# A graph attention layer on one core: ten chunks of edges in place of eleven

## The chip, the cores and the metric

The kernel runs on 1 core of one Trainium2 chip. The metric is the time on the device, in microseconds (us). Three runs of the kernel before gave 5710.31, 5714.75 and 5733.31 us; their median is 5714.75. The profile shows one more execution, recorded by the hardware profiler, which took 5704.97 us, with a span of 5703.2 us from its first to its last instruction.

The engines are called as in the profile: PE is the matrix engine (PEld its weight loads), DVE the vector engine, ACT the scalar engine, POOL the GpSimd engine, SP the engine whose queue issues most transfers. L1192 is line 1192 of the kernel.

## The reference

There are 12500 nodes of 128 features and 412500 edges with 64 features each, sorted by `dst`. The sources `src` are spread at random. Cut to what matters, the reference computes:

```
n      = relu(layernorm(x))                       # 12500 x 128
h,q,k,v = n@Wn+bn, n@Wq+bq, n@Wk+bk, n@Wv+bv
eh     = edge_attr @ We + be                      # 412500 x 128
hmid   = leaky_relu(concat(q[src], k[dst], eh) @ A1 + b1, 0.2)
scores = leaky_relu(hmid @ A2 + b2, 0.2)          # 8 heads
w      = softmax(scores.mean(-1), over all edges)
out    = segment_sum(w[:, None] * v[dst], src)
y      = h + out
result = x + gamma*(y - mean(y))/sqrt(var(y)+eps) + beta
```

The edges come in the order of `dst`, and the sums go by `src`. So the kernel has to bring the edges into another order on the way.

## The kernel before

**The work in tiles.** The edges make 403 *groups* of 1024, and a group has 8 tiles of 128 edges. The nodes, as sources, make 98 *blocks* of 128: the block of an edge is `src` mod 98, its place in the block the quotient.

**The first stage** (`first_stage`, from L953) goes through the groups in order. For a group SP loads the edge features (`ea_t`, L966), a window of 42 nodes' k and v (`kv`, L971) and the edges' positions in that window (`offs`, L974). DVE turns the positions into a selection (`sel`, L984). In four half steps PE multiplies the features by the folded weights (L1007) and adds the selected k and v (L1010), ACT takes the result out of PSUM into a ring of rows (L991, L994), and POOL scatters the rows to a table in DRAM (`tab`, L924), 8 scatters of 128 rows to a group. A row has 257 numbers: the place in the block, 128 of the hidden layer and 128 of v.

**The second stage** (`second_stage`, from L1023) goes through the blocks. The table has room for so many tiles of each block. A *unit* is as many blocks as make at most 12 tiles: three blocks of 4 tiles, four of 3 or four of 2. For a unit SP loads the rows (`rows_of`, L1038), the queries of its blocks (`qw`, L1049) and the spread places (`pls`, L1068). The work goes by *quads* of four tiles. PE turns four tiles (L1088) and adds the queries by a selection (L1093): three matmuls, one for each of three parts of q, and for each block that the quad touches. ACT and DVE make the leaky relu (L1102, L1103). For each unit come the heads (L1110), the scores (L1118 to L1161) and a running maximum. Then DVE builds the weighted selection of each tile (L1179; in the last chunk ACT builds one tile of each quad, L1184 and L1185), PE multiplies it by v (L1192), and DVE adds the sums of the unit to the accumulator of all nodes, faded to the new maximum (L1208).

**Chunks.** So that both stages run at once, the groups are cut into chunks, and each chunk has its own part of the table, three parts in rotation (`TABS`). The table of numbers `CHUNKS` (L72) gives for each chunk its number of groups and the least number of tiles for each block. `tiles_of` (L157) raises that number where the edges still to come would not fit. What a block has beyond the places of its chunk goes on into the next chunk's part. Edges that find no place at all would go through a slow loop over all groups at the end (`other_edges`, L1299); the trace shows none of it.

**Slots.** Before a chunk's edges can be scattered, each needs its slot in the table. `ready(c)` (L641) finds them: `count` makes a histogram of the blocks (L467, L474), `plan` sets what is carried over, and `place_slots` ranks the edges within their blocks (L572, L579, L635), five tile columns at a time.

**The order.** The program is one order for each engine, written by `interleave` (L80): in the loop over stages (L1421 to L1453) stage c mixes the first stage of chunk c, the second stage of chunk c-1 and `ready(c+1)`, each in proportion to its number of steps. Stage 0 has no blocks to work on; there the node projections and the index work of all chunks go beside. After the last chunk's groups only its blocks are left: the *tail*. Two waits tie the stages together: the load of a block's rows waits for the last scatters of its chunk, and the first scatter of a chunk waits until the part of the table that it takes over has been read. At the start of stage 0 zeros are written to places that may stay empty in the second and third part (`clear_ends`, L226).

Of the kernel before, what the change touches and what calls it, by code (L numbers as in the profile page):

```python
# [68 lines left out]
AHEAD = 140  # L69
LEAD = 4  # L70
SURE = 3.75
CHUNKS = ((57, 4), (43, 4), (43, 4), (43, 3), (33, 3), (33, 3), (33, 3), (33, 3), (33, 3), (33, 3), (19, 2))  # L72
BECAUSE = "worked out within these bounds on the chip"


def _ceil(a, b):
    return -(-a // b)
# [44 lines left out]
def kernel(ctx: ExitStack, tc: tile.TileContext, n_edges, x, src, dst, ea, w_nv, w_qt, w_kt,  # L122
# [22 lines left out]
    g0 = 0  # L145
    whole = sum(n for n, _ in CHUNKS)
    for i, (n, _) in enumerate(CHUNKS):
        n = NG - g0 if i == len(CHUNKS) - 1 else max(1, round(NG * n / whole))
        chunks.append((g0, n))
# [4 lines left out]
    for c in reversed(range(NC)):  # L154
        mean = sum(means[c:])
        needed = mean + SURE * mean ** 0.5 - P * sum(tiles_of)
        tiles_of.insert(0, max(_ceil(int(needed) + 1, P), CHUNKS[c][1]))  # L157
    chunks = [(g0, n, t, NTN * t) for (g0, n), t in zip(chunks, tiles_of)]
# [1387 lines left out]
```

## Time and profile before

| | |
|---|---|
| median of three runs | 5714.75 us |
| the profiled execution | 5704.97 us, span 5703.2 us |
| PE busy | 4378.4 us, 77% of the span |
| DVE busy | 4076.2 us, 71% |
| POOL busy | 3239.9 us, 57% |
| ACT busy | 1897.7 us, 33% |
| mean granted clock of PE | 0.879 of full speed |
| moved by DMA | 1316.75 MB, 231 GB/s on the mean |

Busy shares are of the whole span, and the stages differ; the view of stretches gives the same numbers for a stretch of time. A line of the view of groups has the line, engine, operation, names and shapes with their count, then busy time and mean ns of one, then the idle time before them and what ended it. Matmuls overlap in their pipeline, so the sum of their busy time is not the time that PE needs. A scatter's time on POOL is that of issuing it; its transfer comes after.

### The profile page before, as it was taken

Reading aid. Unit: us, or ns where it says so; the run is one execution under the profiler, and the core shown is the slowest. Engines: PE = TensorE matmul, PEld = TensorE weight load, DVE = VectorE, ACT = ScalarE, POOL = GpSimd, SP = SyncE. Lnnn points to the kernel's source line nnn. Section 1 sums busy time; section 2 is a strip of 40 time slices with the busy share of each in tenths; the row PEclk is TensorE's granted clock in tenths of the full one; section 3 lists DMA queues with packets and bytes.
Section 4 is the critical chain, followed back from the end, with each engine's and each line's share of the span. In section 5 each row is a group of like instructions: output and inputs, shape, how many; then the busy total and the mean of one; then the engine's idle time right before and its main releaser. Section 6 shows DMA issues by size and latency. Waiting matters only on the chain. (4 is left out here: it accounts for less than half of the span.)

```text
span 5703.2 us, 86990 instructions
## 1 busy us (share of the span) xinstructions
PE 4378.4 (77%) x26559; PEld 3030.7 (53%) x26559; DVE 4076.2 (71%) x12996; ACT 1897.7 (33%) x5104; POOL 3239.9 (57%) x3250
## 2 busy tenths in 40 slices
PE   6766647877777777777777877778777787778898
PEld 3333324555555555555555555555555555556674
DVE  7777526776777666667776767777777776667898
ACT  2333322333333333333333333333333333333346
POOL 3666566665566555665655655665655665665510
PEclk8888768998898888888888988888989888989999
DMA  4667767777777777776777767777776776778985
GB/s 134 202 196 218 212 208 226 243 246 224 226 241 234 224 225 241 236 234 222 239 227 232 244 224 239 231 242 232 245 236 215 247 237 210 253 236 273 304 280 198
DMA packets 711378, 1316.75 MB, mean 231 GB/s; under 512 B 152208, under 2 KB 362309, under 8 KB 710889
## 3 DMA queue, kind: packets, MB, share of 16 engines
q1 hardware_dynamic: 492080, 867.97, 52.1%
q0 software_dynamic: 154704, 424.26, 20.1%
q10 hardware_dynamic: 64105, 18.76, 1.4%
q8 instruction: 214, 3.51, 0.3%
q14 instruction: 275, 2.25, 0.1%
HBM read 820.50 MB, written 490.10 MB: 230 GB/s over the span
## 5 line engine op out<-in xcount | busy, mean ns | idle before, releaser
L924 POOL DMA_INDIRECT tab<-row,slots x3223 | 3236.7, 1004 | 2211.9 <-ACT row L994 979.8
L1192 PE MATMUL o_ps<-rows_of,w 128*128 128x128 f32 x6860 | 1020.7, 292 | 313.4 <-DVE w L1179 170.0
L1192 PEld LDWEIGHTS o_ps<-rows_of,w 128*128 128x128 f32 x6860 | 913.5, 201 | 440.3 <-issue 258.8
L994 ACT ACTIVATE row<-row_ps 128x512 f32<-128x512 f32 x1151 | 681.2, 593 | 1126.1 <-PE row_ps L1010 343.4
L1102 ACT ACTIVATE low<-h_ps 128x512 f32<-128x512 f32 (+1 forms) x861 | 511.8, 594 | 1438.6 <-remote 432.6
L1007 PE MATMUL row_ps<-w_ea,ea_t 128*128 128x256 f32 x2302 | 821.6, 442 | 188.0 <-ACT row L994 127.0
L1179 DVE TENSOR_SCALAR w<-iota_f,rows_of,score 128x128 f32<-128x128 f32 x3381 | 954.6, 357 | 0.1
L1103 DVE TENSOR_TENSOR rows_of<-h_ps,low 128x512 f32<-128x512 f32 (+1 forms) x861 | 589.1, 684 | 497.5 <-ACT low L1102 335.0
L1093 PE MATMUL h_ps<-sel_q,qw 128*128 128x128 fp8e4 (+3 forms) x4242 | 766.9, 314 | 5.4 <-issue 5.2
L1007 PEld LDWEIGHTS row_ps<-w_ea,ea_t 128*128 128x128 f32 x2302 | 425.8, 214 | 420.9 <-issue 186.3
L1110 PE MATMUL s_ps<-rows_of,a_sb 128*32 128x384 f32 (+2 forms) x2392 | 314.7, 604 | 384.4 <-DVE rows_of L1103 257.2
L1088 PE MATMUL h_ps<-ident,rows_of 128*128 128x128 f32 x3430 | 580.1, 295 | 5.8 <-issue 5.8
L1010 PEld LDWEIGHTS <-sel 126*128 126x128 fp8e4 x3224 | 344.2, 107 | 298.4 <-issue 77.7
L1088 PEld LDWEIGHTS h_ps<-ident,rows_of 128*128 128x128 f32 x3430 | 455.1, 154 | 83.0 <-issue 44.4
L1010 PE MATMUL row_ps<-kv,sel 126*128 126x256 bf16 x2302 | 489.1, 296 | 7.0 <-issue 4.6
L1093 PEld LDWEIGHTS <-qw 128*128 128x128 bf16 x4242 | 412.5, 104 | 134.7 <-issue 39.8
L635 DVE TENSOR_REDUCE num<-run 128x5 f32<-128x490 f32 (+1 forms) x648 | 425.9, 657 | 6.4 <-PE run L579 2.2
L994 ACT ACTIVATE row<-t_bank 128x512 f32<-128x512 f32 x461 | 273.5, 593 | 465.9 <-PE t_bank L1010 190.6
L579 PE MATMUL run<-one,rest_b 128*128 128x500 f16 x637 | 263.1, 413 | 210.8 <-DVE num L635 127.9
L984 DVE TENSOR_SCALAR sel<-offs,third 126x512 fp8e4<-126x512 uint8 x806 | 365.4, 494 | 64.9 <-remote 31.8
L1078 DVE TENSOR_SCALAR sel_q<-pls,part 128x512 fp8e4<-128x512 uint8 (+1 forms) x837 | 367.7, 492 | 0.0
L1148 DVE TENSOR_SCALAR_CACHE_REDUCE s_ps<-s_ps,less_of 128x128 f32<-128x128 f32 x298 | 105.9, 355 | 365.6 <-PE o_ps L1192 114.7
(249 smaller groups left out, 4420.3 us busy)
## 6 DMA issues: line engine op xcount, KB each, us to landing
rows_of<-tab SPq DMA_DIRECT2D x264, 1542.0 KB
ea_t<-in_ea SPq DMA_DIRECT2D x403, 256.0 KB
qw<-q_tab SPq DMA_DIRECT2D x192, 384.0 KB
tab<-row,slots POOLq DMA_INDIRECT x3223
offs<-off_d SPq DMA_DIRECT2D x403, 126.0 KB
pls<-pl_d SPq DMA_DIRECT2D x264, 192.0 KB
rows_of<-tab SPq DMA_DIRECT2D x27, 1028.0 KB
qw<-q_tab SPq DMA_DIRECT2D x96, 288.0 KB
```

Source lines behind the costliest of these rows:

```text
L635: nc.vector.tensor_reduce(num, strips[:, :NTN, :m].rearrange("p b m -> p m b"), AX.X, ALU.max)
L924: i = nc.gpsimd.indirect_dma_start(out=tab[:, :], out_offset=bass.IndirectOffsetOnAxis(ap=slots[c][t // (8 * STR)][:m, t % (8 * STR):t % ( ...
L994: nc.scalar.activation(row[:, :, 1:ROW], bank, AF.Copy)
L1007: nc.tensor.matmul(bank[:, :, 0:D], lhsT=ea_g[:, ts(k, P)], rhs=w_ea, start=True, stop=False, skip_group_check=True)
L1010: nc.tensor.matmul(bank[:, b, :], lhsT=sel[:, ts(b * halves + k, P)], rhs=kv, start=False, stop=True, skip_group_check=True)
L1078: nc.vector.tensor_scalar(sel[:, a:b], plss[i][:, a:b], part1, None, op0=ALU.is_equal, saturate=False)
L1088: nc.tensor.matmul(h_ps[:, ts(j, P)], lhsT=rows_of[i][:, a + j, 1:D + 1], rhs=ident, is_transpose=True, start=j == 0, stop=False, skip_gro ...
L1093: nc.tensor.matmul(h_ps[:, (x0 - a) * P:(x1 - a) * P], lhsT=qws[i][:, s, ts(k, D)], rhs=plss[i][:, x0 * P:x1 * P], start=False, stop=k == ...
L1102: nc.scalar.activation(low, h_ps, AF.Copy, scale=SLOPE)
L1103: nc.vector.tensor_max(rows_of[i][:, a:b, 1:D + 1], h_ps.rearrange("p (j e) -> p j e", j=m), low.rearrange("p (j e) -> p j e", j=m))
L1179: nc.vector.tensor_scalar(w, iota_f, rows_of[i][:, t, 0:1], state["score", i][:, t:t + 1], op0=ALU.is_equal, op1=ALU.mult)
L1192: nc.tensor.matmul(state["o_ps"][:, ts(t // ct, D)], lhsT=w, rhs=rows_of[i][:, t, D + 1:ROW], start=t == 0, stop=t % ct == ct - 1, skip_gr ...
```

## The change

Only the table of chunks changes:

```diff
-CHUNKS = ((57, 4), (43, 4), (43, 4), (43, 3), (33, 3), (33, 3), (33, 3), (33, 3), (33, 3), (33, 3), (19, 2))
+CHUNKS = ((57, 4), (46, 4), (46, 4), (45, 4), (45, 4), (45, 4), (45, 4), (33, 3), (24, 2), (17, 2))
```

The first number is the groups, the second the tiles of a block. Both tables have 403 groups and 35 tiles for each block. Before, three chunks had blocks of four tiles, seven of three and one of two; now it is seven, one and two. Through `interleave` this moves every instruction from stage 1 on. Two places show how.

On PE, in stage 5, a quad of chunk 4 before. Its blocks have three tiles, so a quad touches two blocks:

```order
L1088 MATMUL h_ps<-ident,rows_of 128x128 x4
L1093 LDWEIGHTS qw
L1093 MATMUL h_ps<-sel_q,qw 128x128
L1093 LDWEIGHTS qw
L1093 MATMUL h_ps<-sel_q,qw 128x128
L1093 LDWEIGHTS qw
L1093 MATMUL h_ps<-sel_q,qw 128x128
L1093 LDWEIGHTS qw
L1093 MATMUL h_ps<-sel_q,qw 128x384
L1093 LDWEIGHTS qw
L1093 MATMUL h_ps<-sel_q,qw 128x384
L1093 LDWEIGHTS qw
```

A sixth matmul of 384 columns ends it. With the change a quad there is one block of four tiles:

```order
L1088 MATMUL h_ps<-ident,rows_of 128x128 x4
L1093 LDWEIGHTS qw
L1093 MATMUL h_ps<-sel_q,qw 128x512
L1093 LDWEIGHTS qw
L1093 MATMUL h_ps<-sel_q,qw 128x512
L1093 LDWEIGHTS qw
L1093 MATMUL h_ps<-sel_q,qw 128x512
```

Three matmuls of 512 columns stand for six that have as many columns together.

On SP's queue, late in the program, in the last stage that still has groups. Before this is stage 10, with 19 groups and the blocks of chunk 9, three tiles each (771 numbers of a partition are three rows of 257; `ea_t`, `kv` and `offs` belong to a group, the others to a unit):

```order
L1038 DMA rows_of<-tab 128x4x771
L1068 DMA pls<-pl_d 128x1536
L1049 DMA qw<-q_tab 128x1536
L966 DMA ea_t<-in_ea 128x512
L971 ISA
L971 DMA kv<-kv_tab 126x256
L974 DMA offs<-off_d 126x1024
L1038 DMA rows_of<-tab 128x4x771
```

With the change it is stage 9, with 17 groups and the blocks of chunk 8, two tiles each:

```order
L1038 DMA rows_of<-tab 128x4x514
L1049 DMA qw<-q_tab 128x1536
L1068 DMA pls<-pl_d 128x1024
L1038 DMA rows_of<-tab 128x4x514
L966 DMA ea_t<-in_ea 128x512
L971 ISA
L971 DMA kv<-kv_tab 126x256
L974 DMA offs<-off_d 126x1024
L1049 DMA qw<-q_tab 128x1536
L1068 DMA pls<-pl_d 128x1024
L1038 DMA rows_of<-tab 128x4x514
```

The units there are smaller, two quads instead of three, and a load of the queries belongs to two quads instead of three.

## The prediction

> **What bounds the kernel now.** I read the page first, then the busy time stage by stage, because the change only moves work between stages.
>
> ```profile
> span 5703.2 us, 86990 instructions
> ...
> PEclk8888768998898888888888988888989888989999
> ```
>
> No engine is full over the span, so the stages have to be seen apart. Stage c forms and scatters the rows of chunk c, works on the blocks of chunk c-1 and finds the slots of chunk c+1. Its end is the last scatter of its chunk. The view of stretches below has one row for each stage, from stage 0 to stage 10, then the tail. The columns are the length, then busy time and count on PE, PEld, DVE, ACT and POOL, then clock, DMA share and GB/s. The count on POOL is 8 per group (344 for 43 groups, 264 for 33, 151 for 19).
>
> ```profile
> core 0: us, PE busy (x) PEld busy (x) DVE busy (x) ACT busy (x) POOL busy (x), PEclk, DMA share, GB/s
> 72.00:810.00 738.00, 490.60 (x1714) 245.93 (x1712) 484.99 (x1365) 255.78 (x615) 459.65 (x455) 0.78 0.72 204
> 810.00:1375.00 565.00, 425.28 (x2491) 290.99 (x2492) 381.37 (x1223) 173.17 (x442) 344.68 (x344) 0.88 0.76 235
> 1375.00:1948.00 573.00, 449.46 (x2714) 312.41 (x2712) 418.20 (x1343) 184.03 (x488) 347.24 (x345) 0.90 0.77 233
> 1948.00:2517.00 569.00, 434.36 (x2592) 300.87 (x2589) 386.27 (x1235) 180.33 (x478) 344.07 (x345) 0.88 0.73 233
> 2517.00:2963.00 446.00, 346.74 (x2233) 251.87 (x2233) 320.00 (x1039) 141.80 (x374) 264.64 (x265) 0.89 0.73 231
> 2963.00:3410.00 447.00, 347.84 (x2271) 253.32 (x2272) 322.08 (x1030) 140.94 (x374) 263.37 (x266) 0.89 0.72 232
> 3410.00:3850.00 440.00, 345.04 (x2262) 253.60 (x2261) 320.82 (x1021) 142.00 (x374) 266.44 (x264) 0.89 0.76 235
> 3850.00:4288.00 438.00, 346.76 (x2269) 255.66 (x2262) 320.04 (x1022) 140.83 (x374) 263.10 (x265) 0.88 0.75 237
> 4288.00:4734.00 446.00, 346.23 (x2267) 253.53 (x2263) 320.43 (x1025) 140.63 (x374) 265.79 (x264) 0.88 0.73 232
> 4734.00:5173.00 439.00, 334.81 (x2200) 247.78 (x2196) 286.16 (x907) 139.37 (x374) 263.77 (x265) 0.88 0.74 235
> 5173.00:5451.00 278.00, 247.19 (x1903) 194.02 (x1898) 231.54 (x738) 103.48 (x291) 153.00 (x151) 0.97 0.91 293
> 5451.00:5629.00 178.00, 159.54 (x1379) 128.30 (x1377) 172.50 (x606) 94.07 (x279) 0.99 (x1) 1.00 0.76 250
> ```
>
> Two regimes show. Stages 1 to 9 run at a pace of groups: stages 1 to 3 take 1707 us for 129 groups, 13.23 us each, and stages 4 to 9 take 2656 us for 198, 13.41 each (442.7 us a stage). It is not the slot work that sets it: stage 9 finds slots for 19 groups instead of 33, its DVE time falls by 34 us, and its length stays at 439. Stage 0, with no blocks at all, still takes 738/57 = 12.95 us a group. Stage 10 and the tail are otherwise: 75 quads (batches of four tiles) over 19 groups, then 50 quads and no group, with DVE at 83% and 97%, PE at 89% and 90%, and DMA at 0.91 in stage 10.
>
> In the group regime POOL is the nearest to full, and it waits for its rows:
>
> ```profile
> L924 POOL DMA_INDIRECT tab<-row,slots x3223 | 3236.7, 1004 | 2211.9 <-ACT row L994 979.8 <-issue 861.9 <-ACT plT L1059 166.5
> ```
>
> Scatters take 1.00 us and 861.9/3223 = 0.27 us between, so 8 take 10.2 us of the 13.2. The rest is ACT's row coming late, in a program order that couples PE, ACT, DVE and POOL. I find no single wait that ends all others; the paces are what I cost with.
>
> **The change part by part.** After it, seven chunks have 4 tiles, one 3, two 2: still 35 tiles a block, in 306 units instead of 299 and 858 quads instead of 861 (the schedule keeps 99 places for a four-tile chunk's 98). Stages become (groups, quads, groups whose slots are found): stages 1 and 2 46, 99 (46, then 45); 3 to 5 45, 99, 45; 6 45, 99, 33; 7 33, 99, 24; 8 24, 75, 17; 9 17, 50, 0; then the same tail of 50 quads of two-tile blocks. Stage 0 keeps 57 groups.
>
> *The query matmuls: nothing.* Before, a quad of three-tile blocks needs six, now three; 1176 of some 4250 go. The busy times of the forms seem to promise time:
>
> ```profile
> L1093 PE MATMUL h_ps<-sel_q,qw 128*128 128x512 fp8e4 x882 | 262.1, 409 | 1.1 <-issue 1.0
> L1093 PE MATMUL h_ps<-sel_q,qw 128*128 128x384 fp8e4 x1050 | 257.2, 358 | 1.3 <-issue 1.1
> L1093 PE MATMUL h_ps<-sel_q,qw 128*128 128x256 fp8e4 x1302 | 185.2, 279 | 2.8 <-issue 2.8
> L1093 PE MATMUL h_ps<-sel_q,qw 128*128 128x128 fp8e4 x1008 | 119.1, 230 | 0.3 <-issue 0.2
> ```
>
> By these a four-tile quad costs 262.1/294 = 0.89 us and the others 561.5/567 = 0.99, some 39 us over the 392 quads that change. But the stretch itself, in order of time, first of a three-tile chunk and then of a four-tile one, is equal:
>
> ```profile
> 3009.28 0.82 PE L1093 MATMUL h_ps<-sel_q,qw 128*128 128x128 fp8e4 x6
> ...
> 1376.15 0.81 PE L1093 MATMUL h_ps<-sel_q,qw 128*128 128x512 fp8e4 x3
> ```
>
> The same columns stream. Bounds 0 and 39 us of PE, which is idle over 20% of these stages; I take 0.
>
> *One pass less over the sums and the queries: in the pace.* A chunk reads and rewrites the whole accumulator and reads all queries once:
>
> ```profile
> L1208 DVE SCALAR_TENSOR_TENSOR acc<-acc,fade_of,o_ps 128x512 f32<-128x512 f32 (+3 forms) x290 | 188.7, 657 | 134.3 <-remote 42.3 <-PE row_ps L1010 39.9 <-PE h_ps L1093 18.1
> ```
>
> ```profile
> qw<-q_tab SPq DMA_DIRECT2D x192, 384.0 KB
> qw<-q_tab SPq DMA_DIRECT2D x96, 288.0 KB
> ...
> tab<-blank SPq DMA_DIRECT2D x98, 128.5 KB
> ...
> tab<-blank SPq DMA_DIRECT2D x98, 72.3 KB
> ```
>
> That is 188.7/10 = 19 us of DVE, and 9.4 MB, 98 blocks of 96 KB. Both lie beside work in stages whose length is the groups'; their price, 0 to 19 us, is inside the difference of 13.41 and 13.23 and not counted again. The zeroing in stage 0 falls from 128.5 and 72.3 to 72.3 and 40.2 KB, under a DMA share of 0.72: 0.
>
> *A stage less: 6 us each.* 33 groups at 13.23 are 436.7, so each of stages 4 to 9 has 6.0 us above. It stands at its start. Rows of the same view for the first 70 us of stages 2, 5 and 8 and the rest of two of them:
>
> ```profile
> 1375.00:1445.00 70.00, 51.62 (x312) 34.90 (x311) 45.65 (x165) 18.14 (x46) 41.54 (x42) 0.83 0.68 213
> 1445.00:1948.00 503.00, 397.84 (x2404) 277.52 (x2403) 372.55 (x1180) 165.89 (x442) 305.70 (x303) 0.91 0.78 235
> ...
> 2963.00:3033.00 70.00, 53.80 (x374) 39.12 (x375) 50.28 (x181) 20.67 (x57) 37.52 (x39) 0.88 0.63 199
> 3033.00:3410.00 377.00, 294.05 (x1899) 214.20 (x1898) 271.80 (x850) 120.28 (x318) 225.86 (x228) 0.89 0.74 238
> 4288.00:4358.00 70.00, 53.28 (x361) 38.51 (x358) 47.95 (x174) 20.45 (x56) 37.12 (x37) 0.88 0.63 196
> ```
>
> Later scatters run at 303/503 = 0.60 and 228/377 = 0.60 per us alike; at the start a three-tile stage has 37 to 39 in 70 us where 42 are due, some 7 us lost, a four-tile one 42 and none. By the code the first block load of a chunk stands there on SP's queue until the chunk's last scatters have landed.
>
> *Stages 1 to 6:* 272 groups at 13.23 = 3599. Bounds: with 32 quads fewer than at the old ratio (594 against 626), each at 0.73 (below), 3576; with 7 us lost at each start, 3641.
>
> *Stages 7 to 9* are the unknown: 74 groups with 224 quads, 3 to a group, between the 2.3 of the group regime and the 3.9 of stage 10. Low end: the pace of groups alone, 437 + 318 + 225 = 980. High end: DVE at its share of stage 10, 231.54/278 = 0.83. Its prices need three rows:
>
> ```profile
> L984 DVE TENSOR_SCALAR sel<-offs,third 126x512 fp8e4<-126x512 uint8 x806 | 365.4, 494 | 64.9 <-remote 31.8 <-issue 13.3 <-DMA offs<-off_d 12.1
> L1179 DVE TENSOR_SCALAR w<-iota_f,rows_of,score 128x128 f32<-128x128 f32 x3381 | 954.6, 357 | 0.1
> L1185 ACT ACTIVATE w<-w,score 128x128 f32<-128x128 f32 x49 | 19.7, 401 | 1.6
> ```
>
> A group's selection is 365.4/403 = 0.91 us; finding its slots (320.7 - 286.2)/14 = 2.46; a three-tile quad (231.5 - 17.2)/75 = 2.86; a four-tile one 2.72 (stages 2 and 3, less those); a two-tile one 172.5/50 = 3.45, plus 0.28 where ACT takes no tile, as it does for 49 in the tail only. Stage 7: 269 + 30 + 59 = 358; stage 8: 214 + 22 + 42 = 278; stage 9: 186 + 15 = 202. At 0.83 that is 430, 334 and 242; with 437 for stage 7's groups, 1013. PE and DMA may as well have held stage 10 as DVE, so I take the middle, 441 + 326 + 233 = 1000.
>
> Stage 9 is new in kind: 25 loads of two-tile units among 17 groups, 1.5 to a group on SP's queue instead of 0.8. Its transfers can be summed:
>
> ```profile
> rows_of<-tab SPq DMA_DIRECT2D x264, 1542.0 KB
> ea_t<-in_ea SPq DMA_DIRECT2D x403, 256.0 KB
> ...
> offs<-off_d SPq DMA_DIRECT2D x403, 126.0 KB
> ...
> kv<-kv_tab SPq DMA_DIRECT2D x403, 63.0 KB
> ```
>
> A tile is 1542/12 = 128.5 KB, so a group moves 8 x 128.5 + 445 = 1473 KB, 1.5 MB; the tail's blocks moved at most 178 us x 250 GB/s = 44.5 MB. Together 70 MB in 233 us is 300 GB/s, just what stage 10 moved (293). So I don't go under the middle there.
>
> *Stage 0* finds slots for 3 groups more, 7 us of DVE that is busy 66%: 0 to 7, I take 3. *The sum:* stages 1 to 10 take 4641 now, then 3599 + 1000 = 4599; 42 less, 3 back: 39. From the profiled execution, 5704.97 us, that gives 5666. It lies 10 under the median of the runs, 5714.75; from that, **5676**.
>
> **The rivals.** *The late stages run at the pace of groups* and the early ones at 3576: 3576 + 980 = 4556, 85 less and 3 back: 5633. For it: the clock is 0.97 in stage 10 against 0.88 to 0.90 in stages 1 to 9, and more quads per group would keep PE busier. Against it: DVE would be at 358/437 = 82%, 87% and 90%, over stage 10's.
>
> The Trainium skill's page "TensorE: Matmul & The Clock Gate", in Part 1, says the clock gate starts throttled and is released by sustained activity; that agrees with 0.97 where PE is 89% busy and 0.88 at 78%. By that rule stages 7 to 9 would lean to this rival.
>
> *Every group and quad costs the same anywhere.* Stages 4 to 9 and stage 10 differ by 14 groups and 164.7 us: 11.76 a group, then 0.73 a quad. Groups stay 346, quads in these stages go from 822 to 818: 3 us less and 3 back, 5715. For it: with stage 10 so quick, a move of quads is a mere exchange. Against: it puts stages 1 to 3 at 578 (569) and the tail's 50 quads at 37 (178).
>
> *Slower: the slot work holds DVE at 72%.* In stages 4 to 8 DVE has 320.7/442.7 = 0.72 while it serves PE slot by slot; stage 10 had no slots to find. Were 0.72 the most in stages 7 and 8, they take 497 and 386: 3599 + 1116 = 4715, 74 more and 3: 5792. It costs time once the share stays under 636/806 = 0.79. Against: stage 9, with fewer slots, had no use for the DVE time it gained, so DVE was not what held it.
>
> *It doesn't do what it says:* edges beyond their chunk's places go to the slow loop at the end; 403 passes of 784 tiles at 0.29 us are tens of milliseconds. Against: a block has 4480 places for 412500/98 = 4209 edges, as before.
>
> **How the numbers follow.** The forecast 0.42 (its own range 5650 to 5700), the faster rival 0.18, no gain 0.27, slower 0.11, the slow loop 0.02. What a measurement can tell from no change is about 0.5%, 29 us; three quarters of the forecast's range lie beyond it. Faster 0.32 + 0.18 = 0.50, same 0.10 + 0.27 = 0.37, slower 0.13. The range reaches to both neighbours, 5625 to 5735.
>
> **What would show it.** Stages 1 to 6 at 609 and 595 us, with starts that lose nothing; over 13.3 us a group there the first term is wrong. Stages 7, 8 and 9 at 441, 326 and 233 with a clock of 0.92 or more; at 0.88 and DVE near 72% the slower rival holds. The tail at 178 and stage 0 ending at 810 to 817. PE's idle share in stages 4 to 6 should not fall by the query matmuls' 39 us.

## The result, and the profile after

The changed kernel takes 5678.0 us in the median of five runs (5665.77 to 5690.10), the kernel before 5714.75 (five runs, 5710.31 to 5733.31). The ratio is 0.9931 with a 95% interval of 0.9906 to 0.9956: 0.7% faster, where 5676 was forecast. The profiled execution took 5672.94 us.

One thing has to be said ahead of the rest: the experiments further down ran on three chips of the same type at other levels of time, and on two of them the kernel before takes about 4724 us and not 5715. In this text the chip of the prediction is A (5715 us for the kernel before), the others are B (4724.17), C (4725.44) and D (5627.95). Each ratio is to the kernel before on the same chip. The change as it is was timed on A and C alone. On C it is 1.4% slower; on B two kernels that have it and one edit more are 1.6% slower; on D two kernels with ten chunks, and with tiles moved to ACT besides, are 0.9% faster. So the result holds for A and, for kernels near it, on D, and part of the explanation is why the sign differs.

First the span of the change, and its busy time by stretches: one row for each stage from 0 to 9, then the tail, with the columns of the prediction.

```profile
span 5671.3 us, 84831 instructions
```

```profile
72.00:797.00 725.00, 491.32 (x1732) 247.15 (x1732) 490.00 (x1375) 259.32 (x617) 458.89 (x455) 0.78 0.67 195
797.00:1399.50 602.50, 440.15 (x2556) 301.82 (x2556) 395.63 (x1259) 181.16 (x457) 366.43 (x369) 0.86 0.73 229
1399.50:1999.00 599.50, 459.52 (x2699) 317.09 (x2697) 415.04 (x1319) 186.30 (x491) 369.05 (x368) 0.87 0.73 229
1999.00:2596.00 597.00, 459.06 (x2741) 317.63 (x2740) 421.70 (x1351) 189.88 (x502) 360.90 (x361) 0.88 0.75 229
2596.00:3187.00 591.00, 453.12 (x2743) 315.04 (x2744) 421.87 (x1348) 188.20 (x502) 361.52 (x360) 0.90 0.76 230
3187.00:3779.50 592.50, 457.49 (x2749) 316.16 (x2747) 424.17 (x1357) 188.81 (x502) 359.83 (x360) 0.89 0.75 230
3779.50:4360.00 580.50, 447.51 (x2683) 312.42 (x2682) 396.38 (x1269) 187.71 (x502) 360.46 (x361) 0.89 0.77 235
4360.00:4832.50 472.50, 384.32 (x2448) 271.81 (x2446) 361.52 (x1177) 158.86 (x430) 264.88 (x265) 0.92 0.77 250
4832.50:5186.00 353.50, 294.41 (x2079) 221.03 (x2080) 282.60 (x924) 120.01 (x327) 196.29 (x192) 0.93 0.79 255
5186.00:5417.50 231.50, 184.78 (x1369) 143.73 (x1369) 163.66 (x557) 82.40 (x243) 132.85 (x136) 0.94 0.90 269
5417.50:5598.00 180.50, 160.07 (x1378) 128.69 (x1378) 174.04 (x616) 94.90 (x284) 0.98 (x1) 0.99 0.77 252
```

Stage 0 ends at 797, where it ended at 810 before. Stages 1 to 6 take 3563 us for 272 groups, 13.10 a group. Stages 7 to 9 take 472.5, 353.5 and 231.5, together 1057.5, and DVE is busy 77%, 80% and 71% of them. The tail is 180.5.

The ends of the stages, taken to the last scatter, make the account of the 32 us between the spans, 5703.2 and 5671.3. Take 13.1 us for a group everywhere and look at what each stage has above that:

| chip A | before | change |
|---|---|---|
| stage 0 ends at | 810 | 797 |
| stages with four-tile blocks, 2.2 or 2.3 quads a group | stages 1 to 3: 1707, +17 | stages 1 to 6: 3563, 0 |
| three-tile blocks, 33 groups and 75 quads | stages 4 to 9: 2656, +62 | none |
| 33 groups, 99 quads | none | 472.5, +40 |
| 24 groups, 75 quads | none | 353.5, +39 |
| 17 groups, 50 quads | none | 231.5, +9 |
| 19 groups, 75 quads | 278, +29 | none |
| sum above 13.1 a group | 108 | 88 |

Groups are the same in number, 346. So 13 us come from stage 0, 20 from the stages, and 2 are lost after the last scatter. The 79 us that stages 1 to 9 had above the pace are gone, and 59 of them come back in the last three stages, which have more quads to a group.

### The profile page after: what moved, and what is told of

It is laid out like the page before. It is cut to its first block, busy times and chain, and to the rows that moved or that the text cites. A ratio compares the mean times of both kernels' runs of the same rounds, so it can differ in the third digit from the quotient of the medians.

```text
span 5671.3 us, 84831 instructions
## 1 busy us (share of the span) xinstructions
PE 4336.8 (76%) x25460; PEld 2934.5 (52%) x25460; DVE 4058.9 (72%) x12995; ACT 1898.8 (33%) x5125; POOL 3235.7 (57%) x3249
## 5 line engine op out<-in xcount | busy, mean ns | idle before, releaser
L1192 PE MATMUL o_ps<-rows_of,w 128*128 128x128 f32 x6860 | 1012.8, 291 | 308.2 <-DVE w L1179 162.6
L1192 PEld LDWEIGHTS o_ps<-rows_of,w 128*128 128x128 f32 x6860 | 909.1, 200 | 428.1 <-issue 211.1
L994 ACT ACTIVATE row<-row_ps 128x512 f32<-128x512 f32 x1151 | 680.6, 593 | 1187.2 <-PE row_ps L1010 383.4
L1179 DVE TENSOR_SCALAR w<-iota_f,rows_of,score 128x128 f32<-128x128 f32 x3381 | 955.1, 356 | 0.1
L1102 ACT ACTIVATE low<-h_ps 128x512 f32<-128x512 f32 x858 | 511.2, 596 | 1311.8 <-PE h_ps L1093 366.8
L1103 DVE TENSOR_TENSOR rows_of<-h_ps,low 128x512 f32<-128x512 f32 x858 | 588.3, 686 | 494.7 <-ACT low L1102 306.8
L1007 PE MATMUL row_ps<-w_ea,ea_t 128*128 128x256 f32 x2302 | 815.9, 440 | 153.6 <-ACT row L994 97.0
L1093 PE MATMUL h_ps<-sel_q,qw 128*128 128x512 fp8e4 (+3 forms) x3084 | 749.8, 363 | 8.3 <-issue 5.9
L1007 PEld LDWEIGHTS row_ps<-w_ea,ea_t 128*128 128x128 f32 x2302 | 432.0, 214 | 411.6 <-issue 192.8
L1110 PE MATMUL s_ps<-rows_of,a_sb 128*32 128x384 f32 (+1 forms) x2448 | 323.6, 608 | 406.0 <-DVE rows_of L1103 270.0
L994 ACT ACTIVATE row<-t_bank 128x512 f32<-128x512 f32 x461 | 273.3, 593 | 482.9 <-PE t_bank L1010 142.5
L1093 PEld LDWEIGHTS <-qw 128*128 128x128 bf16 x3084 | 312.9, 103 | 134.0 <-issue 36.2
```

The source lines that it names most:

```text
L994: nc.scalar.activation(row[:, :, 1:ROW], bank, AF.Copy)
L1007: nc.tensor.matmul(bank[:, :, 0:D], lhsT=ea_g[:, ts(k, P)], rhs=w_ea, start=True, stop=False, skip_group_check=True)
L1093: nc.tensor.matmul(h_ps[:, (x0 - a) * P:(x1 - a) * P], lhsT=qws[i][:, s, ts(k, D)], rhs=plss[i][:, x0 * P:x1 * P], start=False, stop=k == ...
L1102: nc.scalar.activation(low, h_ps, AF.Copy, scale=SLOPE)
L1103: nc.vector.tensor_max(rows_of[i][:, a:b, 1:D + 1], h_ps.rearrange("p (j e) -> p j e", j=m), low.rearrange("p (j e) -> p j e", j=m))
L1179: nc.vector.tensor_scalar(w, iota_f, rows_of[i][:, t, 0:1], state["score", i][:, t:t + 1], op0=ALU.is_equal, op1=ALU.mult)
```

## The experiments

Short names: "33/99" is a stage with 33 groups and 99 quads. All kernels compute the whole reference. Where an expectation names levels near 5700 us for a run on B, C or D, it is to be read as a difference from the kernel before.

**1. The two-tile end alone, with eleven chunks (chip B).** The last two chunks are those of the change, the three-tile chunks stay.

```diff
-CHUNKS = ((57, 4), (46, 4), (46, 4), (45, 4), (45, 4), (45, 4), (45, 4), (33, 3), (24, 2), (17, 2))
+CHUNKS = ((57, 4), (46, 4), (46, 4), (46, 4), (34, 3), (34, 3), (33, 3), (33, 3), (33, 3), (24, 2), (17, 2))
```

> Eleven chunks as before, with the change's end alone: (57,4), three of 46 with 4 tiles, 34, 34, 33, 33, 33 with 3, then 24 and 17 with 2; 35 tiles a block. If the gain is that of one stage less, as the prediction has it, this kernel has none: 5700 to 5715 us. If it comes from the two-tile end, it is all here: about 5678 us.

Measured 4796.99 us, ratio 1.0156 (1.0141 to 1.0171): 73 us slower, which neither branch of the expectation had. Taken to the last scatters, stage 0 ends at 733.7; then come 498, 495 and 483 (46 groups), 400.5 (34/99), 365.5, 352, 348, 347 (three-tile blocks), 309 (24/75) and 211 (17/50). At 10.6 us a group the 34/99 stage has 40 us above the pace, 24/75 has 55, 17/50 has 31, the others together some 15; before, on the like chip C, has 60 in all (below).

**2. Ten chunks with the old end (chip B).** Five four-tile stages, then 33 groups three times and 19.

```diff
-CHUNKS = ((57, 4), (46, 4), (46, 4), (45, 4), (45, 4), (45, 4), (45, 4), (33, 3), (24, 2), (17, 2))
+CHUNKS = ((57, 4), (46, 4), (46, 4), (46, 4), (45, 4), (45, 4), (33, 3), (33, 3), (33, 3), (19, 2))
```

> Ten chunks as in the change, with the end of the kernel before: (57,4), three of 46 and two of 45 with 4 tiles, three of 33 with 3, 19 with 2; 35 tiles a block. One stage less as the cause: about 5680 us, as the change. The two-tile end as the cause: 5715 us, as before.

Measured 4779.56 us, ratio 1.0121 (1.0104 to 1.0138). Stage 0 ends at 725.4; 496.5, 493.6, 486.5, 476.0, 475.2; then 399.2 (33/99), 356.3, 345.5, and 260.1 for 19/75. Slower too, and again where many quads meet few groups: 33/99 has 49 us above 10.6 a group, 19/75 has 59. So on B neither the kernel with the new end nor the one with a stage less gains.

**3. The query matmuls cut in two (chip B).** The change, with the three 512-column matmuls of a four-tile quad made into three of 128 and three of 384, as a three-tile quad has them.

```diff
-                for k in range(3):
-                    nc.tensor.matmul(h_ps[:, (x0 - a) * P:(x1 - a) * P], lhsT=qws[i][:, s, ts(k, D)],
-                                     rhs=plss[i][:, x0 * P:x1 * P], start=False, stop=k == 2, skip_group_check=True)
+                for y0, y1 in ([(x0, x0 + 1), (x0 + 1, x1)] if x1 - x0 == 4 else [(x0, x1)]):
+                    for k in range(3):
+                        nc.tensor.matmul(h_ps[:, (y0 - a) * P:(y1 - a) * P], lhsT=qws[i][:, s, ts(k, D)],
+                                         rhs=plss[i][:, y0 * P:y1 * P], start=False, stop=k == 2, skip_group_check=True)
```

> The changed kernel, with the query matmuls of each four-tile quad cut again into 128 and 384 columns: six in place of three in some 686 quads, the same columns and the same sums. If these matmuls cost nothing, as the prediction took it from the order of time: 5678 us within 10. If the busy times of their forms are what they cost (0.1 us a quad): 69 us more, 5747 us.

Measured 4797.35 us, ratio 1.0156 (1.0139 to 1.0172). The change itself stands at 4793.08 and 1.0137 (1.0112 to 1.0162) on C, whose kernel before is equal within 1.3 us; the intervals overlap. The groups of the cut matmuls, and of the whole ones in the change on C:

```profile
L1094 PE MATMUL h_ps<-sel_q,qw 128*128 128x384 fp8e4 x2208 | 494.8, 334 | 1.4 <-DVE sel_q L1078 1.4
L1094 PE MATMUL h_ps<-sel_q,qw 128*128 128x128 fp8e4 x2202 | 250.9, 224 | 19.2 <-DVE sel_q L1078 19.1
```

```profile
L1093 PE MATMUL h_ps<-sel_q,qw 128*128 128x512 fp8e4 x2058 | 573.8, 389 | 21.7 <-DVE sel_q L1078 18.2 <-DMA kv<-kv_tab 3.5
...
L1093 PE MATMUL h_ps<-sel_q,qw 128*128 128x384 fp8e4 x150 | 32.6, 326 | 2.3 <-DVE sel_q L1078 2.3
L1093 PE MATMUL h_ps<-sel_q,qw 128*128 128x128 fp8e4 x144 | 15.9, 219 | 0.0
```

2058 matmuls more stand there, and the busy time of these forms rises from 622 to 746 us; the time differs by about 4. On B itself kernel 4, below, has the whole matmuls and some 10 us more in stage 0, and takes 4796.28 us: the cut ones cost some 10 us at most, not 124. PE's busy time over the whole kernel does not tell them apart: 4050.9 us here, 4042.1 in the change on C, 4054.1 in kernel 4. The sums count what overlaps. That is shown for this kind of chip; on A it was not tried.

**4. The zeros of the kernel before (chip B).** The change, with as many places zeroed in stage 0 as before.

```diff
-        from_slot.append(min(tiles_of[c] * P, 8 * int((mean - SURE * mean ** 0.5) / 8)))
+        from_slot.append(min(tiles_of[c] * P, (512, 440, 384)[c]))
```

> The changed kernel, which writes as many zeros in stage 0 as the kernel before (72 and 128 rows of each block in place of 40 and 72, 8.65 MB more). Stage 0 ended at 810 us before and at 797 with the change. If the zeros are the cause: stage 0 ends at 808 to 812 again and the whole takes 13 us more, 5691 us. If not: stage 0 ends at 795 to 800, 5678 us.

Measured 4796.28 us, ratio 1.0159 (1.0138 to 1.0179). The transfers of zeros in the change (here they are 128.5 and 72.3 KB, as before), and stage 0 here:

```profile
tab<-blank SPq DMA_DIRECT2D x98, 72.3 KB
tab<-blank SPq DMA_DIRECT2D x98, 40.2 KB
```

```profile
71.00:734.00 663.00, 471.71 (x1781) 242.44 (x1779) 496.32 (x1405) 260.03 (x625) 458.92 (x455) 0.82 0.81 228
```

Stage 0 ends at 734.2, and at 724.6 and 725.4 in kernels 3 and 2, which have the change's zeros: some 10 us. The whole stands only 3 us over the change on C, less than the intervals can tell, so how much of it reaches the end stays open. Kernel 1 has the change's zeros and one chunk more to index; its stage 0 ends at 733.7, so a chunk's index work is worth some 9 us too.

**5. Both kernels again (chip C).**

> The kernel before, unchanged, for its stages beside those of the other runs of this call. On a chip like that of the four experiments before, where it took 4724 us: stages 4 to 9 with 33 groups and 75 quads at 345 to 357 us each, as in r2_end_old, and its gain over the ten-chunk kernels (55 to 73 us) in stages 1 to 3. On a chip like that of the prediction, 5715 us: stages 4 to 9 at 438 to 447 us.

> The change, unchanged. If the query matmuls and the zeros cost nothing, it takes what r3_six and r4_zeros took on their chip, 4797 us within 10, there 1.5% more than before; if each of the two edits cost the time by which those kernels were slower than before, 4724 us. On a chip like that of the prediction: 5678 us.

The kernel before took 4722.75 us (ratio 0.9996, 0.9983 to 1.0008), the change 4793.08 (1.0137, 1.0112 to 1.0162). The stretches of before: stages 0, 4 and 10. Then those of the change: stages 0, 4, 7, 8 and 9.

```profile
72.00:747.00 675.00, 480.38 (x1776) 248.56 (x1775) 489.35 (x1393) 260.73 (x626) 458.44 (x455) 0.80 0.80 224
...
2131.00:2481.00 350.00, 309.73 (x2233) 235.20 (x2232) 316.78 (x1031) 143.59 (x371) 269.72 (x264) 0.96 0.90 295
...
4221.00:4475.00 254.00, 223.36 (x1776) 178.12 (x1775) 218.18 (x697) 98.97 (x277) 150.25 (x152) 0.97 0.97 317
```

```profile
72.00:723.00 651.00, 467.51 (x1781) 240.91 (x1779) 495.84 (x1405) 259.73 (x624) 460.62 (x455) 0.83 0.76 218
...
2199.00:2674.00 475.00, 421.70 (x2735) 303.12 (x2736) 418.86 (x1344) 195.31 (x502) 362.34 (x361) 0.94 0.96 287
...
3630.00:4009.00 379.00, 348.33 (x2372) 254.59 (x2370) 348.14 (x1139) 156.33 (x417) 266.80 (x264) 0.97 0.93 307
4009.00:4326.00 317.00, 281.44 (x2083) 215.58 (x2078) 282.51 (x927) 122.62 (x327) 193.95 (x192) 0.97 0.90 288
4326.00:4543.00 217.00, 176.88 (x1368) 141.92 (x1366) 164.44 (x561) 85.08 (x246) 132.21 (x135) 0.94 0.93 281
```

Three-tile stages with 33/75 take 350 us, 10.6 a group, and four-tile stages with 45/99 take 475, 10.6 as well. Here no three-tile stage stands above the pace, so to have fewer of them saves nothing. The last stages do stand above it: 379 for 33 groups is 29 over 10.6 a group, 317 for 24 is 63, 217 for 17 is 37, 129 in all, where before had 53 in its stage 10. Stages 1 to 3 before have +16 (the expectation put its gain over the ten-chunk kernels there; it lies in the late stages), stages 4 to 9 have -9; stages 1 to 6 of the change have +24. That is 93 us more in the stages and 24 less in stage 0, 69 in all; the spans differ by 72.6. So the parts of the change go the same way on both kinds of chip, except for the gain of fewer three-tile stages, which A has and C has not (for D see kernel 10).

**6. The slot work doubled in one place (chip C).** The change, with the comparison that `place_slots` makes for each five columns done twice: 0.465 us of DVE each, 648 times.

```diff
-            nc.vector.tensor_tensor(
-                one[:, :, :m], bins_b[:, :, :m],
-                near[0][:, t0 % batch:t0 % batch + m].unsqueeze(1).to_broadcast([P, NBIN, m]), op=ALU.is_equal)
+            for _ in range(2):
+                nc.vector.tensor_tensor(
+                    one[:, :, :m], bins_b[:, :, :m],
+                    near[0][:, t0 % batch:t0 % batch + m].unsqueeze(1).to_broadcast([P, NBIN, m]), op=ALU.is_equal)
```

> The changed kernel, with the comparison of place_slots (L572, 0.465 us, once for five tile columns) done twice on DVE: 0.74 us more for each group whose slots are found, 34 us in each of stages 1 to 5, 25, 18 and 13 us in stages 6 to 8. If DVE sets a stage's length, the stage grows by that much, 240 us in all; if the pace of scatters or of transfers sets it, by less than a third, under 80 us; stage 9 and the tail don't change.

Measured 4882.42 us, ratio 1.0345 (1.0324 to 1.0366), 89 us over the change, between the two branches of the expectation. Stages 0, 4 and 7:

```profile
72.00:784.50 712.50, 493.04 (x1788) 252.09 (x1787) 570.45 (x1564) 261.29 (x625) 465.36 (x456) 0.81 0.68 200
...
2258.00:2739.00 481.00, 417.67 (x2741) 298.53 (x2740) 449.97 (x1420) 197.19 (x502) 367.93 (x362) 0.96 0.94 284
...
3698.00:4092.50 394.50, 351.27 (x2367) 254.15 (x2365) 365.02 (x1176) 156.79 (x417) 269.19 (x265) 0.97 0.91 296
```

Stage 0 takes 75 us more of DVE and is 61 longer; stages 1 to 6 take some 30 each and are 6 longer all together; stage 7 takes 17 and is 15 longer; stage 8 takes 12 and is 5 longer. The expectation had forgotten stage 0, which has most of the rise. So on this chip the slot work on DVE lies on the path that sets stage 0 and stage 7, and hardly on that of the stages with 2.2 quads a group, where DVE went from 88% to 94% at nearly the same length.

**7. Eight chunks, four of them with six tiles (chip C).** Fewer stages still, and quads per group from 1.4 to 3.9. A straight line through the stages of both traces on A (by the expectation some 17 us a stage, 9.1 a group and 1.3 a quad) makes this faster; a pace of groups with an engine limit makes it slower.

```diff
-CHUNKS = ((57, 4), (46, 4), (46, 4), (45, 4), (45, 4), (45, 4), (45, 4), (33, 3), (24, 2), (17, 2))
+CHUNKS = ((57, 4), (67, 6), (66, 6), (46, 4), (69, 6), (46, 4), (33, 3), (19, 2))
```

> Eight chunks: (57,4), (67,6), (66,6), (46,4), (69,6), (46,4), (33,3), (19,2); 35 tiles a block, all the work as before, two stages less than the change, but the ratio of quads to groups goes 1.5, 2.2, 3.2, 1.4, 3.2, 3.0, 3.9. If a stage costs some 17 us and each group and quad the same anywhere (9.1 and 1.3 us, the best straight fit to the stages of the two traces of the prediction's chip), it takes some 60 us less than the change. If a stage goes at the slower of a pace of groups and a pace of quads, as the prediction has it, the stages of ratio 3 lose more than the others can gain: at least 100 us more than the change.

Measured 5001.49 us, ratio 1.0584 (1.0564 to 1.0604), 208 us over the change. Stage 1 (67/99), stage 3 (46/147) and stage 4 (69/99):

```profile
767.50:1480.50 713.00, 539.18 (x3066) 369.00 (x3066) 467.73 (x1476) 229.52 (x590) 536.13 (x536) 0.87 0.76 238
...
2172.50:2804.00 631.50, 553.51 (x3786) 406.75 (x3783) 582.45 (x1912) 228.26 (x605) 375.48 (x368) 0.96 0.86 261
2804.00:3526.50 722.50, 557.73 (x3282) 393.05 (x3282) 472.40 (x1519) 248.59 (x664) 549.43 (x552) 0.87 0.77 242
```

With 1.4 or 1.5 quads a group the stage stays at 10.6 and 10.5 us a group: it gains nothing from having fewer quads. With 3.2 it takes 13.7 a group, DVE at 92%. So on C a stage reads as the slower of two things: its groups at 10.5 to 10.6, or its work, with DVE, PE or the transfers then some 90% busy (in stage 9 of the change DMA at 0.93). Which of the three it is, these rows do not tell; a stage at the pace of groups has them nearly as busy (stage 4 of the change on C: DVE 88%, PE 89%, DMA 0.96). The straight line falls on this chip; on A and D the eight chunks were not tried.

**8. Tiles from DVE to ACT in the last chunks (chip D).** In the change, ACT builds one tile of each quad in the last four chunks, not in the last one alone (L1184, L1185; the line of `peaks` in the schedule likewise).

```diff
-                if units[i]["c"] == NC - 1 and t == b - 1:
+                if units[i]["c"] >= NC - 4 and t == b - 1:
...
-                if c == NC - 1:
+                if c >= NC - 4:
```

> The changed kernel; in chunks 6 to 9 ACT builds one tile of each quad's weights, as it does in the last chunk alone now (L1184, L1185). DVE has 0.28 us less for each quad, 28, 21 and 14 us less in stages 7 to 9; ACT has 0.79 us more. If DVE's work sets these stages, they shrink by 30, 23 and 15 us, from 379, 317 and 217, and the kernel takes about 4728 us where the change takes 4793. If the transfers set them, or PE, nothing changes but by a few us: 4785 to 4800.

Measured 5580.20 us, ratio 0.9907 (0.9870 to 0.9944). Stages 7 to 9:

```profile
4265.50:4730.00 464.50, 387.24 (x2454) 273.57 (x2453) 342.87 (x1097) 213.90 (x596) 263.31 (x265) 0.93 0.79 254
4730.00:5083.50 353.50, 292.08 (x2070) 219.26 (x2067) 263.32 (x846) 169.64 (x476) 192.54 (x192) 0.94 0.81 255
5083.50:5320.50 237.00, 192.68 (x1378) 147.95 (x1376) 153.37 (x510) 117.43 (x347) 132.76 (x136) 0.91 0.90 265
```

DVE has 19, 19 and 10 us less than in the change on A (28, 21 and 14 were expected). The stages are 464.5, 353.5 and 237.0 long where they were 472.5, 353.5 and 231.5, on a chip that is 1.5% quicker with the kernel before (for 472.5 us that alone is 7). So the stages were hardly waiting for the DVE time taken away. This is read across two chips: the change without the moved tiles was not timed on D.

**9. The same in the kernel before: its last two chunks, and all chunks from chunk 3 on (chip D).** These put to the test whether kernel 8 gained by its tiles and not by the change of chunks. The diff is the first; the second has `>= 3` for `>= NC - 2`.

```diff
-                if units[i]["c"] == NC - 1 and t == b - 1:
+                if units[i]["c"] >= NC - 2 and t == b - 1:
```

> The kernel before; in chunk 9, too, ACT builds one tile of each quad. Only stage 10 has less on DVE, 21 us of 218. If DVE's work sets it: 24 us less, 4700 us where before takes 4724. If the transfers set it (its DMA share is 0.97): 4724.

> The kernel before; in chunks 3 to 10 ACT builds one tile of each quad. If the pace of the scatters sets stages 4 to 9 and DVE only stage 10, it is as the run before, 4700 us. If DVE sets all of them: 22 us less in each of seven stages, 4570 us. If ACT, which evicts the rows, comes too late for its 59 us more in a stage: slower than before.

Measured 5633.99 us, ratio 1.0012 (0.9987 to 1.0036), and 5637.94, ratio 1.0016 (0.9993 to 1.0040). No gain, though in the second DVE has 11 to 20 us less in each of stages 4 to 9; stage 10 takes 273.0 us in both. Stage 5 of the first, where nothing was moved, and of the second:

```profile
2922.00:3358.00 436.00, 343.61 (x2271) 251.66 (x2272) 321.57 (x1029) 140.34 (x374) 265.88 (x264) 0.90 0.74 238
```

```profile
2907.00:3349.50 442.50, 341.16 (x2267) 250.99 (x2264) 303.07 (x953) 189.96 (x522) 262.90 (x266) 0.89 0.73 234
```

**10. Ten chunks with the old end, and tiles on ACT from chunk 5 on (chip D).** The chunks of kernel 2.

```diff
-CHUNKS = ((57, 4), (46, 4), (46, 4), (45, 4), (45, 4), (45, 4), (45, 4), (33, 3), (24, 2), (17, 2))
+CHUNKS = ((57, 4), (46, 4), (46, 4), (46, 4), (45, 4), (45, 4), (33, 3), (33, 3), (33, 3), (19, 2))
...
-                if units[i]["c"] == NC - 1 and t == b - 1:
+                if units[i]["c"] >= NC - 5 and t == b - 1:
```

> Ten chunks with the end of the kernel before (r2_end_old, 4780 us), and ACT building one tile of each quad in chunks 5 to 9. Stage 6 has the quads of a four-tile chunk beside 33 groups, 399 us. If DVE sets stages 6 and 9: 30 and 24 us less, 4726 us, and with stages 7 and 8 at DVE's limit as well 4680. If not: 4780.

Measured 5571.60 us, ratio 0.9910 (0.9874 to 0.9946). Stages 5, 6 (33/99), 7 and 8 (33/75):

```profile
3129.50:3703.50 574.00, 451.52 (x2693) 315.45 (x2691) 395.65 (x1271) 188.09 (x502) 362.14 (x361) 0.89 0.79 237
3703.50:4163.00 459.50, 383.53 (x2485) 272.44 (x2483) 361.56 (x1160) 214.86 (x596) 262.71 (x264) 0.94 0.83 257
4163.00:4600.00 437.00, 344.79 (x2245) 252.02 (x2241) 304.86 (x968) 190.06 (x522) 262.87 (x264) 0.89 0.75 236
4600.00:5032.50 432.50, 335.31 (x2204) 246.23 (x2196) 269.84 (x842) 189.83 (x522) 263.05 (x264) 0.88 0.76 240
```

With either end, ten chunks are 0.9% faster here; moving tiles alone, in the kernel before, did nothing. So on D the gain goes with the ten chunks and not with the two-tile end. On this chip four-tile stages run at 12.8 us a group (574 for 45) and 33/75 at 13.2 (435 for 33): 13 us for each three-tile stage that is no longer there. 33/99 against 33/75 is 459.5 less 434.8, 25 us for 24 quads, 1.0 a quad; 45/99 against 33/99 (574 and 459.5) is 9.5 a group. These are differences of single stages in one trace, and by them each of the three kinds of stage has 46 or 47 us left that is neither group nor quad. Three-tile stages are not all of the gain: stage 0 ends at 802.0 in the first run of kernel 9, at 782.4 in kernel 8 and 787.5 in this one, 15 to 20 of some 50 us.

No version here beats both kernels on both kinds of chip: on B and C the kernel before is the fastest of those timed there, on D kernels 8 and 10 give 0.991, which the change on A (0.9931) is level with.

## Why the prediction was right, and where it was not

The time was right, 5676 against 5678, and the sign was right on A; but three of its terms missed, and that their misses cancel is luck: of the 32 us between the spans 13 come from stage 0, where the prediction had 3 lost. In the profiled execution it summed to 5666, measured 5673.

*The query matmuls: nothing.* Held where it was tried: kernel 3 puts three more into each four-tile quad, which costs some 10 us at most, far from the sums of busy time. On A, PE's idle share in stages 4 to 6 did not fall, as forecast: 22% before, 23% with the change. The Trainium skill's page "TensorE: Matmul & The Clock Gate", in Part 1, gives a fixed cost of about 2.5 ns for each matmul beyond its columns at the full clock; 2058 of them would be 5 us of PE, an estimate; that agrees with some 10 us at most, and no run here can show so little.

*Stage 0: 3 us lost, the zeros at 0.* This step failed: stage 0 ends 13 us earlier on A, 24 on C. The prediction counted the slots of three groups more and priced the zeros by a DMA share that looked loose, and it did not see that a chunk less is also a chunk less to index there. Kernels 4 and 1 priced both on B, some 10 us each. On A the two were not taken apart.

*A stage less, 6 us each, and stages 1 to 6 at 3599.* The direction held, the size was low: 3563, 36 us under the forecast and under its low bound of 3576. The first two stages of 46 groups took 602 and 599, the four of 45 took 597 to 580, against 609 and 595. The starts did not turn out as sharp as the step put it. The first 70 us of stages 2, 3 and 4 of the change, on A:

```profile
1399.50:1469.50 70.00, 49.84 (x302) 32.88 (x300) 42.22 (x154) 17.79 (x46) 44.46 (x45) 0.86 0.73 224
1999.00:2069.00 70.00, 54.04 (x351) 37.59 (x350) 46.72 (x177) 21.45 (x58) 39.84 (x40) 0.89 0.65 201
2596.00:2666.00 70.00, 54.86 (x352) 37.85 (x353) 47.01 (x176) 21.79 (x58) 39.65 (x40) 0.87 0.68 200
```

45, 40 and 40 scatters where 43 are due at 13.1 us a group: stages 3 and 4 lose 4 or 5 us at their start, less than the three-tile ones, but not none. What carries the term is that four-tile stages run at 13.1 (A) and 12.8 (D) a group and 33/75 at 13.4 and 13.2; whether the price belongs to the stage or to the quads is not settled by these runs. The 32 quads fewer than at the old ratio, which the 3599 takes at nothing, would be 32 of the 36 us at kernel 10's 1.0 us a quad; on A that was not tried. On C both have 10.6, and the term is gone.

*Stages 7 to 9 at 1000, at most 1013.* This step failed the other way: 1057.5, 57 us over. The prediction held the stages to be the slower of the groups' pace and DVE at the 83% of stage 10; on A they have DVE at 77%, 80% and 71%, and run at neither limit. What failed is that model: on A and D groups and quads add up. A straight line (14 us a stage, 9.3 a group, 1.3 a quad and 0.8 a group whose slots are found) meets all 19 stages of A's two traces after stage 0 within 9 us, and one without a price of a stage meets them within 10; on C the same form is off by up to 24. On D kernel 10 has 1.0 us a quad and 9.5 a group, and kernels 8 and 9 speak against DVE's time as what stands in the sum. The additive rival had that form, but 11.76 a group and 0.73 a quad, no price of a stage, and stage 0 3 us later; with the same groups and four quads fewer it could only come to 5715. Two steps of the working were off besides. The 441 of stage 7 is not the middle of its bounds, which are both 437. And stage 9 was given 202 us of DVE and had 164: the 3.45 us a quad came from the tail, divided by 50, and from 5452 us on DVE works on 60 quads there (L1103). So it is luck that stage 9 took 231.5 us where 233 was forecast.

The model that failed on A fits C better: there a stage is about the slower of 10.6 a group and 90% of DVE and PE (kernels 6 and 7), though stage 9 of the change has DVE at 76% and PE at 82%. The loss in the late stages, 29, 63 and 37 us where before has 53 in its stage 10, is what makes the change slower there.

*The rivals.* Late stages at the pace of groups (980): no, they took 77 us more on A. DVE held at 72%: no; 77% and 80% on A, 92% in stage 7 on C. The tail (180.5 against 178) and the clock (0.92 to 0.94 in stages 7 to 9) came as forecast. By the Trainium skill's page "TensorE: Matmul & The Clock Gate", Part 1, a busier PE is granted more clock; the trace agrees, 0.92 to 0.94 with PE 80% to 83% busy against 0.86 to 0.90 with 73% to 77% in stages 1 to 6, but the quicker clock did not make these stages as short as the rival that leaned on it.

## What to carry to other kernels

Price a change of schedule stage by stage, as so many groups at a pace and what each stage has above it, and keep that account after the result too: here a total that was right to 2 us hid three terms that were off by 16, 36 and 57. A busy sum over overlapping matmuls, or an engine at 80%, is no price; take a little of that engine's work away, or double it, and see whether the stage moves. And before a gain of under 1% is kept, time it on more than one chip: this one is 0.7% faster on one and 1.4% slower on another.

## What the runs showed of the hardware

That the same program takes 5715, 5628, 4724 and 4725 us on four chips was not expected. (Each chip was met once, and A is told from D by its level alone; so whether the difference belongs to a chip or to its state at the time is open.) POOL's and DVE's instructions last alike on A and C (the tile of L1179 357 and 356 ns); PE's last 3% to 6% longer on A (L1192 292 and 284 ns, L1007 442 and 418). POOL's scatters on C (the prediction shows them on A, 1004 ns and 2211.9 us idle):

```profile
L924 POOL DMA_INDIRECT tab<-row,slots x3223 | 3256.1, 1010 | 1215.8 <-issue 729.7 <-ACT row L994 258.9 <-DMA tab<-row,slots 90.9
```

1010 ns, and 1000 us less idle; busy time and issue are 9.9 us of the 10.6 that a group takes. Of the waits of the kernel before, the rows that differ, on A and then on C (us in total, times, longest):

```profile
POOL tab L924 <- ACT row L994: 979.8, 420, 68.3
...
ACT low L1102 <- remote: 432.6, 100, 9.6
...
ACT row L994 <- remote: 310.1, 106, 13.5
```

```profile
ACT low L1102 <- PE h_ps L1093: 690.5, 587, 7.8
ACT row L991 <- DMA tab<-row,slots: 558.6, 223, 16.5
...
POOL tab L924 <- ACT row L994: 258.9, 271, 67.8
```

On A, ACT stands idle before L1102 and L994 for 743 us for something that the profile calls "remote"; on C no row of "remote" is there at all. The records of the semaphores tell more. In all 206 of these waits the semaphore that came last is one that only PE's instructions raise, so ACT was waiting for PE, and the profile cannot name it because the semaphore came long after the recorded end of a matmul. In one case a quad's last query matmul ends at 3101.38 us by its record; PE's semaphore goes up at 3108.07 and L1102 starts at 3108.09.

Over the whole kernel before, ACT begins L1102 over 0.3 us after both the recorded end of its last matmul and of ACT's own instruction before it in 268 of 861 cases on A, 676 us together, and in 28 of 861 on C, 56 us. In 245 of the 268 it starts within 60 ns of a rise of that semaphore, in none of the 28. The ends of matmuls are modelled in these records, so whether PE itself stood or only its report came late is not shown.

With these gaps POOL waits for its rows, the DMA share is 0.72 to 0.77 in stages 1 to 9 where it is 0.90 and more on C, and the groups take 13.1 to 13.4 us and not 10.6. The granted clock goes with it (0.879 and 0.936 over the span, PE busy 77% and 85%). What makes the gaps stays open. One thing more differs in the records: A's trace of the kernel before holds 52,038 rises of semaphores and C's 119,374, for the same 86990 instructions; kernel 8 on D has 51,196 and kernel 1 on B 119,703. So on A and D who ended a wait is told less surely, and since every timed run here has its span and clock recorded, a part of the recording itself in the longer times is not ruled out.
